# Two-layer graph network: the last steps re-timed, twelve tails shared out anew between VectorE and GpSimd

## The chip, the cores and the metric

The kernel runs on one core of a Trainium2 chip. Its engines are named as in the profile: PE (TensorE; PEld is its weight load), DVE (VectorE), ACT (ScalarE), POOL (GpSimd) and SP (SyncE, which here issues the DMAs). The metric is the device time of one execution in microseconds (us). All data are float32.

## The reference, cut to what matters

There are 128 batches of 128 nodes with 512 features; `adj` is a 128x128 matrix.

```python
# layer 0: A and C are the same product here, so max(relu(A + (C-A))) becomes a row maximum
A = adj @ x;  x = layernorm(x + relu(max_n(A) + b))
# layer 1, 8 heads of 64
q, k, v = split(x @ w_qkv)
attn = softmax(where(adj == 0, -inf, q @ k.T * 64**-0.5))
o = (attn @ v) @ w_proj + b_proj
x = layernorm(x + (o + layernorm(o) * gamma + beta))
```

## The kernel before, in words

Batches go in groups of four (32 groups, g), and a group in two pairs; q numbers the 64 pairs. The order of all work on each engine is written out by hand: every call is pinned, so the Python order is each engine's order, and each engine runs its own list strictly from first to last. The same holds for the DMA list on SP.

**Units.** The products with `w_qkv` and `w_proj` are done for a group at a time as units of seven block products instead of eight (class `Unit`): `product(i)` is one of the seven, 4 matmul calls on PE (8 rows in the trace, 1.73 us), into one of four PSUM banks, b1 to b4. `snap(k)` copies bank b1 to SBUF on ACT (L186, `u_qk`, `u_v`, `u_o`), and `result(half, col)` adds a bank and a snap on DVE (L192) into the unit's output, which frees the bank. There are two qk units, one v unit and one o unit a group. `seed` (L519) puts the projection's bias into a bank ahead of the products. `left_sums` / `run_sums` make the sums of blocks that the products take, on POOL.

**Attention of a batch.** `scores` (16 calls on PE into two PSUM banks, pss0 and pss1, or po and pa), `softmax_max` (scale and mask, L401, and row maximum, L413, on DVE), `softmax_exp` (ACT, L420, one head at a time), `softmax_div` (reciprocal L431 and product L77, DVE), `prob_transpose` (DVE, L441), `prob_write` and `prob_read` (two DMAs over DRAM that finish the transposition: `hop<-pu`, L450, and four `pT<-hop`, L461), then `attend` (PE) and `attend_copy` (ACT, L491).

**Tails.** A batch ends with two layer norms. Statistics: `bn` (L248, L249) on DVE and `finish_stats` (scale `rs` by a power on POOL, shift `sh`); for a few batches `scalar_stats` on ACT. `tail_inner` normalizes o (ACT); `tail_residual` does three POOL operations: times gamma, plus o, plus the layer's input row with beta, which was spilled to DRAM and is reloaded by `tail_reload` (L556) or `tail_reload_one` (L562). `tail_outer` normalizes again (ACT), and a store follows. For some of the last batches `fused_open` (two DVE operations, L619 and L77) and `fused_close` (one, L627) take the place of the inner normalization and of POOL's three.

**Steps.** A loop over pairs p (L772) does in each step: attend of the pair before, scores and softmax of pair p, two units interleaved, layer 0 of a later pair, tails of earlier pairs. It ends with p = LAST = 60. After it the last pairs are written out (L930 to L1136), with L = 127 the last batch. There `scores(L-5)`, `scores(L-4)` begin the first written step and `scores(L-1)`, `scores(L)` begin the third; the last four batches are projected one by one (`last_project`, PE, tile `pp`) with a copy of `w_proj` loaded over the qk weights (`last_load`, tile `wlast`, whose rest takes ten reloaded rows).

Of the kernel before, what the change touches and what calls it, by code (L numbers as in the profile page):

```python
# [9 lines left out]
F32 = mybir.dt.float32  # L10
AF = mybir.ActivationFunctionType
ALU = mybir.AluOpType
# [4 lines left out]
def kernel(  # L17
# [58 lines left out]
    def tt(eng, dst, a, b, op):  # L76
        pin(eng.tensor_tensor(dst, a, b, op))  # L77
# [84 lines left out]
    class Unit:  # L162
# [25 lines left out]

        def result(self, half, col):
            bank, k = {(0, 0): (2, 1), (0, 1): (3, 2), (1, 0): (4, 3), (1, 1): (3, 3)}[half, col]  # L190
            pin(
                nc.vector.tensor_tensor(  # L192
                    self.out[half, col], self.banks[bank], self.snaps[k], ALU.add
                )
            )
# [55 lines left out]
    def finish_stats(mv, keys, eng=None, fused=0):  # L251

        n = len(keys)
        if n == 0:
            return
        sh = small.tile([P, NC], F32, tag="sh", name=f"sh_{mv.name}")
        if eng is None:
            pin(nc.vector.tensor_scalar(sh[:, :n], mv[:, :n, 0], -1.0, None, ALU.mult))
        rs = small.tile([P, NC], F32, tag="rs", name=f"rs_{mv.name}")
        pin(nc.gpsimd.tensor_scalar(rs[:, :n], mv[:, :n, 1], EPS, None, ALU.add))  # L260
        tt(nc.gpsimd, rs[:, :n], rs[:, :n], mhalf.to_broadcast([P, n]), ALU.pow)
        if eng is None:
            tt(nc.gpsimd, sh[:, :n], sh[:, :n], rs[:, :n], ALU.mult)
        elif n > fused:

            part = slice(fused, n)
            pin(eng.tensor_scalar(sh[:, part], mv[:, part, 0], -1.0, None, ALU.mult))
            tt(eng, sh[:, part], sh[:, part], rs[:, part], ALU.mult)
        for k, key in enumerate(keys):
            stat_of[key] = rs[:, k : k + 1], sh[:, k : k + 1]  # L270
# [247 lines left out]

    def seed(unit, bank):  # L519
        cols = slice(HE, D) if bank == 3 else slice(0, HE)  # L520
        bias = bp_bc[:, cols].unsqueeze(1).to_broadcast([P, 2, HE])
        pin(nc.scalar.copy(unit.new_bank(bank), bias))
# [37 lines left out]
    def tail_reload_one(b, place):  # L560
        rs_[b] = place
        pin(nc.sync.dma_start(out=place, in_=spill[b // 2][:, b % 2]))  # L562
# [71 lines left out]
    def stats(name, *items, eng=None, fused=0):  # L634

        mv = small.tile([P, NC, 2], F32, tag="mv", name=f"mv_{name}")
        for k, (kind, b) in enumerate(items):
            bn({"o": o_of, "z": zs.get, "y": xs.get}[kind](b), mv, k)
        finish_stats(mv, items, eng, fused)
        return mv  # L640
# [131 lines left out]
    for p in range(LAST + 1):  # L772
# [117 lines left out]
        if p == 0:  # L890
            xsums = x_sums(1)
            run_sums(xsums[:3])
            second = qk_unit(1, 0)
        elif p == LAST:
            second = qk_unit(g + 1, 1)
        else:
            second = v_unit(g + 1) if ph else o_unit(g - 1)
# [21 lines left out]
        if p == 1:  # L919
            weight_sums(wp, 0, HE)  # L920
        if f is not None:
            one("y", xs, f)
# [6 lines left out]

    L = B - 1  # L930
    po_pa = ("po", "pa")
    pool = nc.gpsimd
# [4 lines left out]
    before.snap(3)  # L937
    attend_copy(L - 7)
    attend(L - 6, "pa")
    attend_copy(L - 6)  # L940
    seed(o_u, 2)
    scores(L - 5)
    scores(L - 4, po_pa)
    before.result(1, 1)
    tail_inner(B // 2 - 7)
    softmax_max(L - 5)
    before.result(1, 0)
    softmax_max(L - 4)
    o_u.product(1)
    o_u.snap(1)  # L950
    o_u.product(2)
    softmax_exp(L - 5)
    seed(o_u, 4)
    o_u.result(0, 0)
    before.product(3)
    before.result(0, 1)
    tail_residual(B // 2 - 7)
    softmax_exp(L - 4, range(4))
    o_u.product(6)
    scores(L - 3)  # L960
    scores(L - 2, po_pa)
    o_u.snap(2)
    seed(o_u, 3)
    softmax_exp(L - 4, range(4, H))
    softmax_div(L - 5)
    prob_move(L - 5)
# [3 lines left out]
    softmax_max(L - 3)  # L970
    softmax_exp(L - 3, range(4))
    o_u.snap(3)
    softmax_exp(L - 3, range(4, H))
    softmax_div(L - 4)
    prob_move(L - 4)
    softmax_max(L - 2)
    o_u.result(1, 1)
    o_u.result(1, 0)
    tail_outer(B // 2 - 8)
    tail_store(B // 2 - 8)  # L980
    tail_reload(B // 2 - 6)
    wlast, room = last_load()
    for t in range(L - 9, L + 1):
        tail_reload_one(t, room[:, t - L + 9])
    v_u.product(2)
    v_u.product(1)
    v_u.snap(1)
    stats("last_1", ("o", L - 9), ("o", L - 8), eng=pool)
    softmax_exp(L - 2, range(4))
    o_u.product(3)  # L990
    o_u.result(0, 1)
    v_u.result(0, 0)
    v_u.product(6)
    v_u.snap(2)
    softmax_exp(L - 2, range(4, H))
    for t in (L - 9, L - 8):
        tail_inner_one(t)
    tail_residual_one(L - 9)
    v_u.product(5)
    v_u.product(7)  # L1000
    stats("last_2", ("o", L - 11), ("o", L - 10), eng=pool)
    tail_residual_one(L - 8, [0])
    softmax_div(L - 3)
    prob_transpose(L - 3)
    prob_write(L - 3)
    v_u.snap(3)
    v_u.product(4)
    v_u.result(1, 1)
    softmax_div(L - 2)
    prob_transpose(L - 2)  # L1010
    prob_write(L - 2)
# [8 lines left out]
    scores(L - 1)  # L1020
    scores(L, po_pa)
    run_sums(o_sums(NG - 2))
    o_u = o_unit(NG - 2)
    seed(o_u, 2)
    for t in (L - 11, L - 10):
        tail_inner_one(t)
    softmax_max(L - 1)
    v_u.result(1, 0)
    v_u.product(3)
    softmax_max(L)  # L1030
    softmax_exp(L - 1, range(4))
    o_u.product(1)
    o_u.snap(1)
    seed(o_u, 4)
    softmax_exp(L - 1, range(4, H))
    v_u.result(0, 1)
    o_u.product(2)
    seed(o_u, 3)
    o_u.product(6)
    o_u.snap(2)  # L1040
    o_u.result(0, 0)
    softmax_exp(L, range(4))
    tail_residual_one(L - 8, [1, 2])
    stats("last_3", ("z", L - 13), ("z", L - 12), ("z", L - 9), eng=pool)
    o_u.product(5)
    o_u.product(7)
    softmax_exp(L, range(4, H))
    o_u.snap(3)
    o_u.product(4)
    softmax_div(L - 1)  # L1050
    prob_move(L - 1)
    o_u.result(1, 1)
    softmax_div(L)
    prob_move(L)
    tail_residual_one(L - 11)
    tail_residual_one(L - 10)
    tail_outer(B // 2 - 7)
    tail_store(B // 2 - 7)
    tail_outer_one(L - 9)
    last_seed(L - 3, "b2")  # L1060
# [3 lines left out]
    attend_copy(L - 2)  # L1064
    o_u.result(1, 0)
    mv = small.tile([P, NC, 2], F32, tag="mv", name="mv_last_4")
    bn(o_of(L - 5), mv, 0)
    bn(o_of(L - 4), mv, 1)
    finish_stats(mv, [("o", L - 5), ("o", L - 4)], pool)
    o_u.product(3)  # L1070
    o_u.result(0, 1)
    last_project(L - 3, wlast)
    for t, tag in ((L - 2, "b4"), (L - 1, "b3"), (L, "b1")):
        last_seed(t, tag)
# [3 lines left out]
    stat = scalar_stats(L - 8, L - 11)  # L1078
    finish_scalar_stats(stat)
# [5 lines left out]
    last_project(L, wlast)  # L1085
    mv = small.tile([P, NC, 2], F32, tag="mv", name="mv_last_5")
    keys = [("o", L - 3), ("o", L - 6), ("o", L - 7)]
    for k in (2, 1, 0):
        bn(o_of(keys[k][1]), mv, k)
    finish_stats(mv, keys, pool, fused=2)  # L1090
    fused_open(L - 3, mv[:, 0, 0:1])
    fused_open(L - 6, mv[:, 1, 0:1])
    fused_close(L - 3)
    tail_residual_one(L - 5)
    for t in (L - 8, L - 11):
        tail_outer_one(t)
    tail_inner_one(L - 7)
    mv = small.tile([P, NC, 2], F32, tag="mv", name="mv_last_6")
    keys = [("o", L - 2), ("z", L - 3), ("z", L - 10)]
    bn(zs[L - 3], mv, 1)  # L1100
    bn(zs[L - 10], mv, 2)
    fused_close(L - 6)
    bn(o_of(L - 2), mv, 0)
    finish_stats(mv, keys, pool, fused=1)
    fused_open(L - 2, mv[:, 0, 0:1])
    fused_close(L - 2)
    for t in (L - 3, L - 10):
        tail_outer_one(t)
    tail_residual_one(L - 4)
    mv = small.tile([P, NC, 2], F32, tag="mv", name="mv_last_7")  # L1110
    keys = [("o", L - 1), ("z", L - 2), ("z", L - 5), ("z", L - 6)]
    for k in (3, 2, 1, 0):
        bn((o_of if k == 0 else zs.get)(keys[k][1]), mv, k)
    finish_stats(mv, keys, pool, fused=1)
    fused_open(L - 1, mv[:, 0, 0:1])
    for t in (L - 2, L - 6, L - 5):
        tail_outer_one(t)
    tail_residual_one(L - 7)
    fused_close(L - 1)
    mv = small.tile([P, NC, 2], F32, tag="mv", name="mv_last_8")  # L1120
    keys = [("o", L), ("z", L - 1), ("z", L - 4)]
    for k in (2, 1, 0):
        bn((o_of if k == 0 else zs.get)(keys[k][1]), mv, k)
    finish_stats(mv, keys, pool, fused=1)
    fused_open(L, mv[:, 0, 0:1])
    for t in (L - 1, L - 4):
        tail_outer_one(t)
    fused_close(L)
    mv = small.tile([P, NC, 2], F32, tag="mv", name="mv_last_9")
    bn(zs[L], mv, 0)  # L1130
    finish_stats(mv, [("z", L)], pool, fused=1)
    mv2 = small.tile([P, NC, 2], F32, tag="mv", name="mv_last_10")
    bn(zs[L - 7], mv2, 0)
    finish_stats(mv2, [("z", L - 7)], pool)
    tail_outer_vector(L, mv[:, 0, 0:1])
    tail_outer_one(L - 7)  # L1136
# [41 lines left out]
```

## Time and profile before

| | us |
|---|---|
| median of 3 runs (lowest, highest) | 1964.25 (1963.17, 1967.03) |
| the profiled execution | 1965.37 |
| its span in the profile | 1963.5 |
| busy: PE, DVE, POOL, ACT | 1935.3, 1561.6, 1297.2, 1061.6 |
| SP's issuing of the ten row reloads (from 1899.24) | 7.50 |
| start of the last store's issue | 1960.35 |

Times in the profile count from the span's start. A timeline row gives start, duration, engine, line of the kernel, operation, tiles written and read with their shapes, how many such operations follow each other (x), and in brackets how long the engine was idle before, and what ended that. A row's duration on DVE or POOL includes the time in which the instruction had begun but waited inside its engine.

### The profile page before, as it was taken

To read this page: it belongs to the slowest core of one execution; us is meant where nothing else is said; L and a number is where in the kernel's file an instruction comes from. 1 tells how busy PE (TensorE), PEld (TensorE's weight loads), DVE (VectorE), ACT (ScalarE), POOL (GpSimd) and SP (SyncE) were. 2 spreads that over 40 slices of the span, in tenths; PEclk is the share of its full clock that TensorE was granted. 3 is DMA by queue.
4 is the path that set the end of the run, shared out by engine and by line. 5 is a ranking of instruction groups with operands and counts; after the bars stand their busy time and mean duration, and the time that the engine had idled before them with its cause. 6 is when DMAs were issued, how large, how long until landed. Compare 5 with 4: busy or idle time off the path is not lost.

```text
span 1963.5 us, 33034 instructions
## 1 busy us (share of the span) xinstructions
PE 1935.3 (99%) x11533; PEld 1637.7 (83%) x11533; DVE 1561.6 (80%) x2513; ACT 1061.6 (54%) x3084; POOL 1297.2 (66%) x827
## 2 busy tenths in 40 slices
PE   9999999999999999999999999999999999999995
PEld 6888888888888888888888888888888888888873
DVE  6767878878778778788787787787887877877876
ACT  3444654655555546546555555455465555554564
POOL 6336766767666767667676667676676766676748
PEclk9999999999999999999999999999999999999998
DMA  7647557576576676675675765765756657667554
GB/s 226 171 119 189 148 175 193 156 189 173 166 196 163 167 200 161 171 186 163 188 181 161 195 162 167 207 156 168 193 158 187 175 169 193 166 168 194 141 182 139
DMA packets 445653, 341.73 MB, mean 174 GB/s; under 512 B 276912, under 2 KB 378416, under 8 KB 445488
## 3 DMA queue, kind: packets, MB, share of 16 engines
q1 hardware_dynamic: 445056, 338.85, 63.3%
q8 instruction: 91, 1.49, 0.3%
q10 hardware_dynamic: 432, 0.79, 0.1%
q14 instruction: 74, 0.61, 0.1%
HBM read 172.82 MB, written 166.72 MB: 173 GB/s over the span
## 4 chain that ended last, share of the span: by engine, by line
PE 96%; DVE 2%; POOL 1%; ACT 1%; DMA 1%; issue 0%; SPq 0%; POOLq 0%; DVEq 0%; ACTq 0%
PE b_qk L74 40%; PE b_v L74 19%; PE b_o L74 18%; PE pss L74 6%; PE po L74 6%; PE pa L74 5%; PE pp L74 0%; DMA wlast<-spill 0%; ACT s L420 0%; POOL zl L77 0%; DVE s L401 0%; DVE s L77 0%; POOL rs_mv_last L77 0%; DVE st_mv_last L248 0%; DVE pu L441 0%
## 5 line engine op out<-in xcount | busy, mean ns | idle before, releaser
L74 PE MATMUL b_qk<-s_x,wqk 128*128 128x256 f32 x2048 | 473.2, 379 | 0.2 <-DVE v L192 0.2
L74 PEld LDWEIGHTS b_qk<-s_x,wqk 128*128 128x128 f32 x2048 | 389.0, 190 | 54.1 <-DVE v L192 0.6
L420 ACT ACTIVATE s<-s,nmax 128x128 f32<-128x128 f32 x1024 | 396.2, 391 | 5.7 <-DVE nmax L413 5.7
L74 PE MATMUL b_qk<-x1T,wqk 128*128 128x256 f32 x1536 | 358.9, 383 | 0.1
L74 PEld LDWEIGHTS b_qk<-x1T,wqk 128*128 128x128 f32 x1536 | 286.6, 190 | 45.3 <-issue 1.0
L77 POOL TENSOR_TENSOR z<-z,ga_bc 128x1024 f32<-128x1024 f32 x58 | 164.7, 2839 | 169.2 <-ACT z L274 169.2
L260 POOL TENSOR_SCALAR rs_mv<-mv 128x6 f32<-128x6 f32 (+2 forms) x61 | 14.6, 239 | 380.9 <-DVE mv L249 380.9
L77 DVE TENSOR_TENSOR s<-s,rec 128x1024 f32<-128x1024 f32 x128 | 252.0, 1969 | 4.4
L186 ACT COPY u_qk<-b_qk 128x512 f32<-128x512 f32 x192 | 112.4, 585 | 245.7 <-PE b_qk L74 244.7
L74 PE MATMUL b_v<-wv,s_x 128*128 128x256 f32 x1024 | 236.9, 379 | 0.0
L74 PE MATMUL b_o<-wp,s_o 128*128 128x256 f32 x992 | 229.7, 379 | 4.0 <-POOL s_o L77 2.6
L74 PEld LDWEIGHTS b_v<-wv,s_x 128*128 128x128 f32 x1024 | 194.4, 190 | 26.6
L74 PEld LDWEIGHTS b_o<-wp,s_o 128*128 128x128 f32 x992 | 188.2, 190 | 30.7 <-POOL s_o L77 3.0
L192 DVE TENSOR_TENSOR qk<-b_qk,u_qk 128x512 f32<-128x512 f32 x256 | 168.2, 676 | 56.6 <-PE b_qk L74 44.4
L401 DVE SCALAR_TENSOR_TENSOR s<-pss,mask 128x512 f32<-128x512 f32 x256 | 164.3, 684 | 59.0 <-PE pss L74 58.8
L77 POOL TENSOR_TENSOR x<-x,be_bc 128x1024 f32<-128x1024 f32 x64 | 181.3, 2834 | 33.4 <-DVE rec L431 27.3
L192 DVE TENSOR_TENSOR v<-b_v,u_v 128x512 f32<-128x512 f32 x128 | 87.1, 681 | 136.9 <-PE po L74 132.1
L420 ACT ACTIVATION_READ_ACCUMULATOR s<-s,nmax 128x1 f32 x1024 | 194.4, 190 | 0.0
L186 ACT COPY u_v<-b_v 128x512 f32<-128x512 f32 x96 | 56.2, 585 | 235.8 <-PE b_v L74 235.8
L186 ACT COPY u_o<-b_o 128x512 f32<-128x512 f32 x93 | 54.4, 585 | 237.0 <-PE b_o L74 237.0
L74 PE MATMUL b_v<-wv,x1T 128*128 128x256 f32 x768 | 176.2, 379 | 0.0
L74 PEld LDWEIGHTS b_v<-wv,x1T 128*128 128x128 f32 x768 | 145.9, 190 | 32.2 <-issue 13.6
(121 smaller groups left out, 3398.8 us busy)
## 6 DMA issues: line engine op xcount, KB each, us to landing
hop<-pu SPq DMA_DIRECT2D x128, 512.0 KB, 3.4
pT<-hop SPq DMA_DIRECT2D x512, 128.0 KB, 3.7
spill<-x SPq DMA_DIRECT2D x64, 512.0 KB, 4.8
x<-in_x_dram SPq DMA_DIRECT2D x62, 512.0 KB, 4.4
xhop<-xt SPq DMA_DIRECT2D x248, 128.0 KB, 2.2
x1T<-xhop SPq DMA_DIRECT2D x248, 128.0 KB, 3.9
xr<-spill SPq DMA_DIRECT2D x59, 512.0 KB, 3.6
out_dram<-xr SPq DMA_DIRECT2D x58, 512.0 KB, 4.1
```

Source lines behind the costliest of these rows:

```text
L74: pin(nc.tensor.matmul(*args, **kwargs))
L77: pin(eng.tensor_tensor(dst, a, b, op))
L186: pin(nc.scalar.copy(t, self.banks[1]))
L192: nc.vector.tensor_tensor(self.out[half, col], self.banks[bank], self.snaps[k], ALU.add)
L260: pin(nc.gpsimd.tensor_scalar(rs[:, :n], mv[:, :n, 1], EPS, None, ALU.add))
L401: nc.vector.scalar_tensor_tensor(s[:, par], pss[b][par], SCALE, mask.unsqueeze(1).to_broadcast([P, NP, P]), ALU.mult, ALU.add,)
L420: nc.scalar.activation(prob[b][:, i], prob[b][:, i], AF.Exp, bias=nmax[b][:, i : i + 1], accum_out=psums[b][:, i : i + 1],)
```

## The change

- The step of pair LAST is taken out of the loop and written out. In it `scores(L-5)`, `scores(L-4)` now come after `product(6)` of its first unit; `scores(L-3)`, `scores(L-2)` and `scores(L-1)`, `scores(L)` move into the next step. All softmax steps of these pairs follow them; `prob_read` is parted from `prob_write` and put later (for L-1 and L behind the store of pair 57).
- Reloads: pairs 59 and 60 go to a new tile `early` in the step of LAST, as whole pairs; pairs 61 to 63 go beside `wlast` as whole pairs. Before, ten single rows went there.
- Units of the last steps: `relay` copies bank b1 to a new bank b2 (ACT) and `product(2)` adds to it; `relayed` copies b2 to the output (ACT). They replace `snap(1)` and `result(0, 0)`, and bank 1 is seeded with the bias, bank 3 with the difference `bd` of the bias' halves, which POOL makes once in step p = 1.
- Tails: L-11, L-10 and L-7 become fused (DVE); outer statistics on ACT are now of L-9, L-8 and L-4 (before L-8 and L-11). The negated means are made on DVE (before, in the tails, on POOL). `stats` computes its items from last to first, everywhere. The order of the tails is new; L-7 no longer comes last.

```diff
-    def finish_stats(mv, keys, eng=None, fused=0):
+    def finish_stats(mv, keys, fused=0):
...
+        def relay(self):
+            pin(nc.scalar.copy(self.new_bank(2), self.banks[1]))
+        def relayed(self):
+            pin(nc.scalar.copy(self.out[0, 0], self.banks[2]))
...
     def seed(unit, bank):
-        cols = slice(HE, D) if bank == 3 else slice(0, HE)
-        bias = bp_bc[:, cols].unsqueeze(1).to_broadcast([P, 2, HE])
+        bias = {1: bp_bc[:, :HE], 3: bd}[bank].unsqueeze(1).to_broadcast([P, 2, HE])
...
-    def stats(name, *items, eng=None, fused=0):
+    def columns(name, *items):
         mv = small.tile([P, NC, 2], F32, tag="mv", name=f"mv_{name}")
-        for k, (kind, b) in enumerate(items):
+        for k, (kind, b) in reversed(list(enumerate(items))):
...
-    for p in range(LAST + 1):
+    for p in range(LAST):
...
+    first.product(6)
+    scores(L - 5)
+    scores(L - 4, po_pa)
+    softmax_exp(L - 6, range(4))
...
+    early = sb.tile([P, 4, D], F32, tag="x1T", name="early", bufs=2)
+    for q in range(2):
+        tail_reload_to(LQ - 4 + q, early[:, ds(2 * q, 2)])
...
+    prob_out(L - 2)
+    softmax_exp(L - 1, range(4, H))
+    v_u.relayed()
+    softmax_max(L)
+    o_u.result(1, 0)
+    o_u.result(0, 1)
...
+    for t in (L - 11, L - 10):
+        fused_open(t, mv2[:, t - L + 11, 0:1])
+    for t in (L - 11, L - 10):
+        fused_close(t)
+    tail_residual_one(L - 8)
+    o_u.product(5)
+    o_u.product(7)
+    o_u.snap(3)
+    last_seed(L - 2, "b1")
+    stats("last_3", ("z", L - 13), ("z", L - 12), ("z", L - 11), ("z", L - 10))
     attend(L - 3)
     attend_copy(L - 3)
     attend(L - 2, "pa")
     attend_copy(L - 2)
+    tail_outer(LQ - 6)
+    tail_store(LQ - 6)
+    prob_read(L - 1)
+    prob_read(L)
+    o_u.result(1, 1)
     o_u.result(1, 0)
...
+    stat = scalar_stats(L - 4)
+    finish_scalar_stats(stat)
+    fused_close(L - 1)
+    tail_outer_one(L - 4)
+    mv8 = stats("last_8", ("o", L), ("z", L - 1), fused=1)
+    fused_open(L, mv8[:, 0, 0:1])
+    tail_outer_one(L - 1)
+    fused_close(L)
```

`prob_out(b)` is `softmax_div`, `prob_transpose` and `prob_write`; LQ = 63 is the last pair.

## The prediction

> **What bounds the kernel now.** I read the page's busy shares and the chain that ended last, then the timelines of PE, DVE, POOL and ACT over the last 120 us, where the change lies, then its first 40 us.
>
> ```profile
> PE 1935.3 (99%) x11533; PEld 1637.7 (83%) x11533; DVE 1561.6 (80%) x2513; ACT 1061.6 (54%) x3084; POOL 1297.2 (66%) x827
> PE 96%; DVE 2%; POOL 1%; ACT 1%; DMA 1%; issue 0%; SPq 0%; POOLq 0%; DVEq 0%; ACTq 0%
> ```
>
> Up to 1891 us PE has no gap after the start; the change removes no matmul, so only gaps and the end can move. The PE timeline has four gaps:
>
> ```profile
> 1891.96 1.97 PE L74 MATMUL b_o<-wp,s_o 128*128 128x256 f32 x8 [1.04 <-DVE o L192]
> 1912.70 1.99 PE L74 MATMUL b_o<-wp,s_o 128*128 128x256 f32 x8 [2.60 <-POOL s_o L77]
> 1915.00 3.72 PE L74 MATMUL b_o<-wp,s_o 128*128 128x256 f32 x16 [0.31 <-ACT b_o L522]
> 1932.46 1.97 PE L74 MATMUL po<-pT,v 128*64 128x128 f32 x16 [3.73 <-DMA pT<-hop]
> 1934.36 12.74 PE L74 MATMUL pp<-wlast,oT 128*128 128x512 f32 x24
> ```
>
> They sum to 7.68 us. The last row shows a further cost: 24 projections in 12.74 us, where 8 took 3.45 in the chain (10.35 for 24). The granted clock was 0.83 and 0.76 in the last two stretches of the table by windows. After the last projection (1947.1) some 16 us remain, held by DVE with short waits for POOL:
>
> ```profile
> 1872.67 0.69 DVE L192 TENSOR_TENSOR qk<-b_qk,u_qk 128x512 f32<-128x512 f32 x1 [7.47 <-PE pss L74]
> 1940.27 0.70 DVE L248 BATCH_NORM_STATS2 st_mv_last<-pp 128x6 f32<-128x512 f32 x1 [3.13 <-PE pp L74]
> 1955.22 0.75 DVE L627 SCALAR_TENSOR_TENSOR z<-z,rs_mv_last,wlast 128x512 f32<-128x512 f32 x1 [1.80 <-POOL rs_mv_last L77]
> 1957.93 0.55 DVE L644 TENSOR_SCALAR z<-z,mv_last,rs_mv_last 128x512 f32<-128x512 f32 x1 [0.22 <-POOL rs_mv_last L77]
> 1959.51 0.81 ACT L274 ACTIVATE zl<-zl,sh_mv_last,rs_mv_last 128x512 f32<-128x512 f32 x1 [1.63 <-POOL sh_mv_last L77]
> ```
>
> DVE idles 7.47 us while PE works (room for a softmax), but is nearly dense from 1883 to 1900. The last store is that of L-7, issued at 1960.35.
>
> The price on which most hangs stands at the kernel's start, where DVE adds SBUF tiles while POOL adds SBUF tiles:
>
> ```profile
> 21.50 1.64 DVE L77 TENSOR_TENSOR s_x<-s_x,x1T 128x512 f32<-128x512 f32 x1
> 23.06 1.75 DVE L77 TENSOR_TENSOR s_x<-x1T 128x512 f32<-128x512 f32 x1
> 24.74 1.75 DVE L77 TENSOR_TENSOR s_x<-x1T,s_x 128x512 f32<-128x512 f32 x1
> 1930.62 0.69 DVE L77 TENSOR_TENSOR wlast<-o,wlast 128x512 f32<-128x512 f32 x1
> 1936.43 1.83 POOL L77 TENSOR_TENSOR zl<-zl,o 128x512 f32<-128x512 f32 x1
> ```
>
> The same DVE operation costs 0.69 us alone and 1.75 beside a busy POOL; POOL's usual 1.27 became 1.83 when a fused close (L627, 0.72 us from 1936.42) stood ahead of it.
>
> **What the Trainium skill says.** "SBUF — State Buffer", section "Who interferes with whom": a DVE instruction with two SBUF inputs and a GpSimd instruction that reads SBUF exclude each other, and the later one waits for the whole of the earlier. The five rows agree. That DVE's scalar_tensor_tensor waits as tensor_tensor does is not shown before the change; that POOL waits for it is. "TensorE: Matmul & The Clock Gate", section "What's actually happening": after an idle window of about 3.4 us PE drops to half clock until it has been busy for about as long. The trace agrees: after 3.73 us of idling the next projections take 0.85 us a row pair instead of 0.43.
>
> **The change, part by part.** I laid the instructions of both orders out engine by engine: each starts when its engine is free and what it reads is there, with the rows' durations. For the order before, this gives gaps of 1.0, 2.5, 0.6, 0.7 and 3.4 us against the measured 1.04, 2.60, 0.31, 0 and 3.73, so a gap is good to about 0.7 us.
>
> *Start.* `stats` now runs its items backwards. For batches 4 to 7:
>
> ```profile
> 28.34 3.31 ACT L292 ACTIVATE x<-x,r 128x512 f32<-128x512 f32 x4 [1.30 <-DVE r L289]
> 30.75 0.68 DVE L248 BATCH_NORM_STATS2 st_mv_second<-x 128x6 f32<-128x512 f32 x1
> ```
>
> DVE began batch 4 at 30.75; batch 7 is written at 31.65, so the four pairs (0.80 each) shift by 0.9 us. The result behind them ended at 34.8, and PE's product(3) at 34.90 needs its bank: **+0.8 us**. For batches 2 and 3 both rows are written (13.91) before DVE comes (14.04): 0. The new bd operation (128x256, under 1 us on POOL) hides beside PE: 0.
>
> *Softmax ahead.* scores(L-5), (L-4) (1.99 us of PE) move one step up, with 7.4 us of DVE per pair of maxima and first division; they fill DVE's 7.47 us hole. The layout leaves one gap, 0.6 us, behind ACT, where normalize(xr) and an exp stand ahead of snap(1). The gaps of 1.04, 2.60 and 0.31 go: **-3.95**. DVE is late next. From exp(L-3)'s end it owes two divisions with transposes (2 x 2.75), two maxima (2 x 2.44) and three results (1.9): 12.3 us, until o_u.result(0,1). PE has the rest of product(7) (1.5), scores 2.0 and four products (6.9), 10.4 us, and then v_u.product(5) needs the bank: gap 1.9. v_u.product(3) waits for a result after attend (0.8), the next product(4) for one behind the division of L, itself 0.9 us late from POOL's sums (0.7). **New gaps 4.0**: this part nets to nothing.
>
> *relay/relayed.* Three DVE results (0.68) go; three ACT copies (0.585) come, two seeds go. Where product(2) now waits for the copy, another product (1.73) covers it: 0. If that cover were gone, 3 x 0.6.
>
> *Reloads.* Ten 256 KB reloads become five of 512 KB, two of them a step sooner. SP spent 7.50 us issuing the ten; PE waited 2.60 through POOL's late residual, counted above. SP's hop writes get free; no DMA in the layout then holds PE until the last pair. There prob_read(L-1), (L) now stand on SP behind the store of pair 57, which waits for ACT's outer normalization and that for last_3. With last_3's statistics out at 1926.8 (worked from the next item): POOL 1.7, ACT 1.6, store 0.4, reads at 0.43 each, landing 3.3 after a pair's last: 1935.2 and 1936.9 against 1932.33 before. PE, at half clock, comes to them at 1935.9, so 0.5 us at most shows.
>
> *Tails.* L-11, L-10 and L-7 go from POOL (nine operations of 1.27) to DVE (three opens of 0.67+0.60, three closes of 0.67: 5.8 alone); one statistics pair goes to ACT (-0.8). L-11 and L-10 stand on DVE ahead of last_3 and of o_u.result(1,1), with POOL busy on L-9 and L-8: 6 x 1.75 = 10.5 us. From one instant (v_u.result(1,0)): DVE 0.6 + 10.5 + 4 x 0.80 + 0.7 = 15.0; PE 5 x 1.73 + 1.9 = 10.6. So PE's product(3) waits **4.4 us**. PE ended its attend at 1922.3 before; now 1922.3 + 0.8 - 3.95 + 4.0 = 1923.2, and product(3) starts at 1927.6 instead of 1922.3. The idle time is over 3.73, so the half clock comes here instead of at the attend.
>
> *End.* From 1927.6 DVE owes 2 results 1.2, 14 statistics pairs 11.2, 6 opens 7.6, 5 closes 3.4, 5 means 0.5, hand-overs 0.9: 24.8; waits for POOL at five of these 5.1, for the slow product(3) 1.1: 31.0, until 1958.6. The scale of L then waits 2.8 behind the scalar statistics of L-4 on POOL (ACT makes them after three outer normalizations); close, statistics, scale, outer 3.4: store at 1964.8. In the old order the last store was issued at 1960.35: **+4.4 us**.
>
> So the span is 1963.5 + 4.4 = 1967.9; that execution took 1965.37, 1.87 more than its span, and the median is 1964.25, 1.1 below it. From the median: **1968.6 us**. A measurement here can tell 0.2% (3.9 us) from no change.
>
> **Rivals.** (A) *PE sets the end, faster.* If DVE's fused operations do not wait for POOL, POOL's steps slip instead and the six take 3.9 us: the 4.4 us gap goes, and with it the half clock (12.74 - 10.35 and 1.0 at the attend: 3.4) and the 5.1 us of waits. PE ends near 1947.1 + 0.8 + 0 - 3.73 - 3.4 = 1940.8, and DVE, behind it by 1.5 to 3 us, ends 4 us sooner than now: 1960.3. It decides from a mean under 1.1 us for these six. For: no row shows scalar_tensor_tensor waiting. Against: tensor_tensor waits, and the skill makes it a matter of inputs.
> (B) *No difference.* If POOL is done earlier or half the operations pass, at 1.2 us each the six take 3.3 us less and the tail loses 2.5 less: 4.4 - 5.8 = -1.4, 1962.9.
> (C) *Worse.* DVE 3% slower over its 70 dense us (2 us) and the half clock reaching the later projections (2 us): 1972.6.
> That the softmax does not in fact come ahead, because its banks are held, would show as PE gaps near 1853; but the maxima that free the banks (L401) end at 1848.2 in that step already.
>
> **How the numbers follow.** The forecast case 0.44, C 0.10, B 0.25, A 0.21: faster 0.21, same 0.25, slower 0.54. The range goes from A's middle to C's middle, 1960.0 to 1973.0, leaving out half of A and of C. The forecast's own range is 1967 to 1971.
>
> **What would show it.** Right: PE gap of 4 to 5 us ended by DVE o before the last b_o product; DVE z/zl rows near 1.75 us ahead of it; product at double time after it; the close of L waiting over 2 us for POOL; a gap of about 0.8 us near 35 us. Wrong: those DVE rows near 0.7, or the last projection ending before 1944.

## The result, and the profile after

The changed kernel took **1969.3 us** (median of 10 runs, 1968.16 to 1970.5) against 1964.31 us for the kernel before in the same series (10 runs): ratio 1.0025, 95% interval 1.0015 to 1.0035. It is slower by some 5 us, a quarter of a per cent; 1968.6 was predicted, with a range from 1960.0 to 1973.0. The profiled execution of the changed kernel took 1970.11 us, its span is 1968.3 us.

The page after, busy times and the chain of work that ended last, shows the same number of matmuls, and a chain with 94% of PE where it had 96%, 3% of DVE where it had 2%, and less than half a per cent of POOL where it had 1%.

```profile
PE 1936.0 (98%) x11533; PEld 1638.4 (83%) x11533; DVE 1576.0 (80%) x2523; ACT 1061.9 (54%) x3087; POOL 1285.9 (65%) x808
PE 94%; DVE 3%; ACT 1%; issue 0%; DMA 0%; POOL 0%; SPq 0%; POOLq 0%; DVEq 0%; ACTq 0%
```

The timeline of PE in the last 102 us of the changed kernel (start, duration, operation, how many, in brackets PE's idle time before and what ended it):

```profile
1866.47 3.76 PE L74 MATMUL b_qk<-s_x,wqk 128*128 128x256 f32 x16 [0.51 <-ACT u_qk L186]
...
1900.92 3.72 PE L74 MATMUL b_v<-wv,s_x 128*128 128x256 f32 x16 [1.78 <-DVE o L199]
1909.12 1.99 PE L74 MATMUL b_v<-wv,s_x 128*128 128x256 f32 x8 [0.86 <-DVE v L199]
1913.33 3.69 PE L74 MATMUL b_o<-wp,oT 128*128 128x256 f32 x16 [0.48 <-DVE v L199]
...
1928.13 3.75 PE L74 MATMUL b_o<-wp,s_o 128*128 128x256 f32 x8 [4.03 <-DVE o L199]
...
1937.18 1.09 PE L74 MATMUL po<-pT,v 128*64 128x128 f32 x16 [1.15 <-DMA pT<-hop]
1939.45 1.09 PE L74 MATMUL po<-pT,v 128*64 128x128 f32 x16 [1.18 <-ACT oT L495]
1940.47 10.57 PE L74 MATMUL pp<-wlast,oT 128*128 128x512 f32 x24
```

The gaps of 1.04, 2.60 and 0.31 us of the order before are gone. In their place stand four small gaps (3.63 us in all), one of 4.03 us that DVE ends, and behind it a product at about half clock (3.75 us for eight rows; 1.99 in the row of 1909.12; the granted clock is 0.54 between 1926 and 1930 us). PE is through at 1951.0, and 14 us of DVE's and POOL's work follow.

DVE's timeline in the same kernel tells why the gap of 4.03 us is there and what the end waits for; three rows of POOL's timeline follow:

```profile
1913.70 1.76 DVE L624 SCALAR_TENSOR_TENSOR zl<-o,mv_last,ga_bc 128x512 f32<-128x512 f32 x1
1915.39 1.75 DVE L77 TENSOR_TENSOR xr<-o,xr 128x512 f32<-128x512 f32 x1
...
1920.42 3.44 DVE L632 SCALAR_TENSOR_TENSOR zl<-zl,rs_mv_last,xr 128x512 f32<-128x512 f32 x2
...
1931.91 0.69 DVE L199 TENSOR_TENSOR o<-b_o,u_o 128x512 f32<-128x512 f32 x1 [1.39 <-PE b_o L74]
...
1961.71 0.77 DVE L632 SCALAR_TENSOR_TENSOR z<-z,rs_mv_last,wlast 128x512 f32<-128x512 f32 x1 [2.60 <-POOL rs_mv_last L77]
```

```profile
1914.88 1.71 POOL L77 TENSOR_TENSOR zl<-zl,ga_bc 128x512 f32<-128x512 f32 x1
1916.67 1.60 POOL L77 TENSOR_TENSOR zl<-zl,o 128x512 f32<-128x512 f32 x1
1918.34 1.60 POOL L77 TENSOR_TENSOR zl<-zl,early 128x512 f32<-128x512 f32 x1
```

The opens and closes of L-11 and L-10, six operations, take about 1.75 us each (one starts every 1.68 us) while POOL has the residual of L-9 and L-8 under way, whose steps are longer too; the statistics of `last_3` and the result that PE needs stand behind them. The last DVE row is the close of L, held 2.60 us by POOL.

### The profile page after: what moved, and what is told of

The parts are those of the page before. It is cut to its first block, busy times and chain, and to the rows that moved or that the text cites. A ratio compares the mean times of both kernels' runs of the same rounds, so it can differ in the third digit from the quotient of the medians.

```text
span 1968.3 us, 33018 instructions
## 1 busy us (share of the span) xinstructions
PE 1936.0 (98%) x11533; PEld 1638.4 (83%) x11533; DVE 1576.0 (80%) x2523; ACT 1061.9 (54%) x3087; POOL 1285.9 (65%) x808
## 4 chain that ended last, share of the span: by engine, by line
PE 94%; DVE 3%; ACT 1%; issue 0%; DMA 0%; POOL 0%; SPq 0%; POOLq 0%; DVEq 0%; ACTq 0%
PE b_qk L74 39%; PE b_v L74 19%; PE b_o L74 18%; PE pss L74 6%; PE po L74 6%; PE pa L74 5%; DVE st_mv_last L255 0%; ACT s L424 0%; DMA x<-in_x_dram 0%; DVE s L77 0%; DVE zl L632 0%; DVE zl L624 0%; DVE pu L445 0%; DVE amax L291 0%; DVE xr L77 0%
```

## The experiments

All were run in five rounds with the kernel before beside them. Executions differ by up to 1.5 us before the first row that this change touches, so the table gives, beside the times, a **stretch** of each profile: from the start of PE's 16 products `b_qk<-x1T` near 31 us (32.07 in the changed kernel) to the start of the last store's issue (1965.02). All of the change lies within it but the order of the first statistics (near 13 us, where DVE waits for no row); a random start does not.

| kernel | median, us | kernel before beside it | ratio (95%) | stretch, us | stretch against the changed kernel |
|---|---|---|---|---|---|
| before | | | | 1928.93 | -4.02 |
| changed | 1969.3 | 1964.31 | 1.0025 (1.0015 to 1.0035) | 1932.95 | |
| statistics forward | 1968.73 | 1964.58 | 1.0021 (1.0013 to 1.003) | 1931.91 | -1.04 |
| L-4 behind L | 1966.88 | 1964.58 | 1.0014 (1.0007 to 1.002) | 1930.13 | -2.82 |
| POOL later | 1968.09 | 1964.58 | 1.0019 (1.0012 to 1.0027) | 1931.53 | -1.42 |
| PE kept busy | 1968.91 | 1964.58 | 1.0022 (1.0013 to 1.0031) | 1931.54 | -1.41 |
| PE early | 1967.68 | 1963.75 | 1.0021 (1.0014 to 1.0027) | 1930.88 | -2.07 |
| three edits | 1964.32 | 1963.75 | 1.0005 (0.9997 to 1.0013) | 1927.95 | -5.00 |
| three edits and POOL's order | 1962.21 | 1963.75 | 0.9992 (0.9984 to 1.0) | 1925.56 | -7.39 |
| the same, results before maxima | 1960.42 | 1963.75 | 0.9982 (0.9974 to 0.999) | 1923.62 | -9.33 |
| before, statistics reversed | 1965.62 | 1964.61 | 1.0007 (0.9999 to 1.0015) | 1927.54 | |
| changed, results before maxima | 1967.28 | 1964.61 | 1.0013 (1.0007 to 1.002) | 1930.06 | -2.89 |

One edit moves the median by less than the interval is wide, so the sizes below are read from the stretches, and the medians agree in direction. Each stretch is one execution, and the last section shows how far executions with the same gap differ. The profiled execution of the changed kernel was 0.8 us over its median, and differences of the ratios give savings that are 0.2 to 1.3 us smaller than those of the last column; PE early comes to 0.8 us by them, PE kept busy to 0.6. The profiled execution of before was itself 1.1 us over its median; differences to before are therefore taken from the ratios.

**Statistics forward.** Theory: DVE is late from the start by the wait for the last of four rows.

```diff
-        for k, (kind, b) in reversed(list(enumerate(items))):
+        order = list(enumerate(items))
+        for k, (kind, b) in order if name in ("first_2", "second", "third") else reversed(order):
```

> The changed kernel with the statistics of the three calls at the start (first_2, second, third) again in the order of their batches. Theory (the reversed order costs at the start and nothing between takes it up): DVE can begin with batch 4 when its row is written, 0.9 us before that of batch 7; PE's gap of 0.79 us at 36.48 us goes, and the end moves by as much, since neither PE nor DVE has room to spare later: span 1968.3 - 0.8 = 1967.5 us, about 1968.5 us in time. Rival (the start is taken up by a later wait): the gap goes at 36 us, but the time stays at 1969.3.

In the timeline of the changed kernel, first 40 us, the wait and the gap that follows from it:

```profile
32.34 0.69 DVE L255 BATCH_NORM_STATS2 st_mv_second<-x 128x6 f32<-128x512 f32 x1 [0.85 <-ACT x L296]
36.48 5.45 PE L74 MATMUL b_qk<-s_x,wqk 128*128 128x256 f32 x24 [0.79 <-DVE qk L199]
```

With the forward order the same PE row has no bracket:

```profile
34.39 5.45 PE L74 MATMUL b_qk<-s_x,wqk 128*128 128x256 f32 x24
```

The row starts 3.48 us into the stretch instead of 4.41, which is 0.93 us less (the bracket shows 0.79 of it), and the stretch is 1.04 us shorter. As expected: what is lost in the first 40 us is still lost at the end, since PE has next to nothing to wait for between (0.23 us, at 70 us).

**Statistics reversed in the kernel before.** The same line, put into the kernel before alone.

```diff
-        for k, (kind, b) in enumerate(items):
+        for k, (kind, b) in reversed(list(enumerate(items))):
```

> The kernel before with one line of the change alone: the statistics of a call to stats run from its last item to its first. Theory: at the start DVE waits 0.85 us for the row of batch 7 (as in the changed kernel), PE gets a gap of 0.8 us before the product behind the results, and the time rises by 0.8 us, ratio 1.0004; the later calls read rows that are all there. Rival (nothing): no such wait, ratio 1.0000. The times can hardly tell 0.8 us; the rows of the first 40 us can.

The timeline of that kernel has the same two waits:

```profile
32.56 0.69 DVE L248 BATCH_NORM_STATS2 st_mv_second<-x 128x6 f32<-128x512 f32 x1 [0.85 <-ACT x L292]
36.71 5.45 PE L74 MATMUL b_qk<-s_x,wqk 128*128 128x256 f32 x24 [0.79 <-DVE qk L192]
```

The waits are the line's doing. The time (ratio 1.0007, interval 0.9999 to 1.0015) agrees and cannot tell 0.8 us, as was expected.

**L-4 behind L.** What POOL does for L-4 stands behind the scales of L.

```diff
     stat = scalar_stats(L - 4)
-    finish_scalar_stats(stat)
     fused_close(L - 1)
-    tail_outer_one(L - 4)
     mv8 = stats("last_8", ("o", L), ("z", L - 1), fused=1)
+    finish_scalar_stats(stat)
     fused_open(L, mv8[:, 0, 0:1])
     tail_outer_one(L - 1)
+    tail_outer_one(L - 4)
```

> The changed kernel with the last three small steps of the scalar statistics of L-4 on POOL, and the outer normalization and store of L-4, put behind the scales of L. Theory: in the changed kernel the last close waits 2.60 us for rs of L, which POOL makes behind L-4's steps, and these wait for ACT; without that the last store is issued at 1965.02 - 2.60 = 1962.4, span 1965.7, time about 1966.7 us. Rival 1 (L-4 takes over as the last): ACT ends L-4's statistics at 1959.4, POOL's 0.3 + 0.9 for L and 0.9 for L-4 stand behind, then ACT 0.8 and the store 0.3: about 1962.6, so no more than 0.3 us less of a gain. Rival 2 (the close is held by DVE's own work or by PE): the wait shrinks but the end moves by less than 1 us.

DVE's timeline, the close of L:

```profile
1957.86 0.75 DVE L632 SCALAR_TENSOR_TENSOR z<-z,rs_mv_last,wlast 128x512 f32<-128x512 f32 x1 [0.46 <-DVE wlast L77]
```

The wait of 2.60 us is 0.46, which is 2.14 less, and the stretch is 2.82 shorter. Another 0.53 goes with a shorter wait of DVE for PE's slow product (0.86 us in this execution, 1.39 in the other), which the edit does not touch. L-4's store is issued at 1960.16, ahead of that of L at 1961.13, so L-4 does not take over. Rivals 1 and 2 are out.

**POOL later.** POOL's six residual steps are moved away from DVE's six operations, which stay.

```diff
-    tail_residual_one(L - 9)
     for t in (L - 11, L - 10):
         fused_open(t, mv2[:, t - L + 11, 0:1])
     for t in (L - 11, L - 10):
         fused_close(t)
-    tail_residual_one(L - 8)
...
     stats("last_3", ("z", L - 13), ("z", L - 12), ("z", L - 11), ("z", L - 10))
+    for t in (L - 9, L - 8):
+        tail_residual_one(t)
```

> The changed kernel with POOL's six residual steps of L-9 and L-8 moved behind the scales of last_3, so that POOL does nothing large while DVE makes the opens and closes of L-11 and L-10. Theory (it is POOL's steps beside them[...] that make six operations take 10.38 us; DVE is the bound): the six come to 4 x 0.67 + 2 x 0.60 = 3.9 us, 6.5 less; the result is there at 1921, before PE asks at 1924.1: the gap of 4.03 goes and product(3) takes 1.97 us, not 3.75; the last projection ends 4 to 7 us earlier. POOL is late next: six steps of 1.27 (7.6 us) now stand ahead of the scales of last_4 and last_5, the first closes begin at about 1935.5 instead of 1939.68, and waits for POOL grow; so the end comes 1 to 4 us earlier, span 1964 to 1967. Rival 1 (PE sets the end): the end follows PE, 5 to 7 us earlier, span 1961 to 1963. Rival 2 (these operations are slow by themselves, in SBUF, with or without POOL): they stay near 1.7 us, the gap stays at 4, and the end comes later by POOL's lateness.

DVE's timeline:

```profile
1913.17 1.76 DVE L624 SCALAR_TENSOR_TENSOR zl<-o,mv_last,ga_bc 128x512 f32<-128x512 f32 x1
1914.85 0.68 DVE L77 TENSOR_TENSOR xr<-o,xr 128x512 f32<-128x512 f32 x1
...
1916.72 1.40 DVE L632 SCALAR_TENSOR_TENSOR zl<-zl,rs_mv_last,xr 128x512 f32<-128x512 f32 x2
...
1937.67 1.76 DVE L632 SCALAR_TENSOR_TENSOR zl<-zl,rs_mv_last,early 128x512 f32<-128x512 f32 x1 [4.91 <-POOL rs_mv_last L77]
```

POOL's timeline, the end of its rest beside them:

```profile
1921.54 0.23 POOL L269 TENSOR_SCALAR rs_mv_last<-mv_last 128x4 f32<-128x4 f32 x1 [7.16 <-DVE mv_last L256]
```

The same operations come to 0.68 to 0.74 us, all but the first, which still meets POOL's last sum for the o unit (1913.11 to 1914.38). So it is POOL's work beside them and not the operation or its operands: rival 2 is out. PE's gap and its slow product are gone, and PE ends 4.1 us earlier in its stretch, but the end gains 1.42 us only. Where the rest went is the last row: POOL's steps now stand ahead of the scales that the first closes need, and DVE waits 4.91 us. Rival 1 (PE sets the end) would have had the end follow PE, 4.1 us here.

**PE kept busy.** Seven matmul calls (14 rows) without use in the gap of 4.03 us.

```diff
     prob_read(L)
+    warm = psum.tile([P, D], F32, tag="pss1", name="warm")
+    for _ in range(7):
+        pe(warm[:, :HE], lhsT=wp[:, 0, 0, :P], rhs=wp[:, 0, 1], start=True, stop=True)
     o_u.result(1, 1)
```

> The changed kernel with seven more matmuls of 128x256, into a bank that is free and whose result nobody reads, in PE's gap of 4.03 us, so that PE's longest idle time there is about 1.1 us. Theory (the half clock comes from the idle time, and DVE is the bound): product(3) takes 1.97 us instead of 3.75 and the next eight projections 3.45 instead of 4.36; DVE's wait of 1.39 us for product(3) goes, and as DVE is dense from there on the end comes 1.0 to 1.4 us earlier, span about 1967.1. PE itself gains nothing at its end, since its next attend waits for reads that land at about 1937. Rival 1 (PE sets the end): PE's end stays at 1951, since the reads hold it, and the end moves by less than 0.3 us. Rival 2 (product(3) is slow for another reason than the idle time): it still takes 3.7 us, and nothing moves.

PE's timeline:

```profile
1924.12 3.29 PE L74 MATMUL warm<-wp 128*128 128x256 f32 x14
1928.21 1.97 PE L74 MATMUL b_o<-wp,s_o 128*128 128x256 f32 x8 [0.81 <-DVE o L199]
...
1936.87 1.97 PE L74 MATMUL po<-pT,v 128*64 128x128 f32 x16 [3.27 <-DMA pT<-hop]
```

The product behind the gap, product(3), takes 1.97 us. PE itself gains nothing by it, since it now waits 3.27 us instead of 1.15 for the reads of L-1, and its last row starts at 1940.71; but DVE's wait of 1.39 us for the product is gone, and the stretch is 1.41 shorter. Here the half clock cost what DVE waited for it.

**PE early.** Both things that hold PE in the last 45 us are taken away: the two results go ahead of the statistics of `last_3`, and the reads ahead of the store of pair 57.

```diff
+    o_u.result(1, 1)
+    o_u.result(1, 0)
     stats("last_3", ("z", L - 13), ("z", L - 12), ("z", L - 11), ("z", L - 10))
...
-    tail_outer(LQ - 6)
-    tail_store(LQ - 6)
     prob_read(L - 1)
     prob_read(L)
-    o_u.result(1, 1)
-    o_u.result(1, 0)
+    tail_outer(LQ - 6)
+    tail_store(LQ - 6)
```

> The changed kernel with o_u.result(1,1) and result(1,0) ahead of the statistics of last_3 on DVE, and the reads of L-1 and L ahead of the store of pair 57 on SP: both things that hold PE in the last 45 us are taken away, while DVE keeps every operation. Worked from the rows of the changed kernel: the two results end 1.3 us after the last close (1923.9) less their overlap, so PE's product(3) starts near 1924.6 at full clock, its eight projections end near 1930, the reads have landed, and 24 projections (10.6 us) end near 1943.5 instead of 1951.0. Theory (DVE is the bound): DVE loses only its wait of 1.39 us for product(3); the end comes 1.4 us earlier, 2.5 at most if POOL's steps meet fewer of DVE's: span about 1966.5. Rival (PE sets the end): the end follows PE by 5 to 7.5 us, span 1961 to 1963.

PE's last row in that kernel's timeline:

```profile
1930.55 10.57 PE L74 MATMUL pp<-wlast,oT 128*128 128x512 f32 x24
```

PE ends at 1941.1, in its stretch 8.7 us earlier than in the changed kernel, and the end comes 2.07 us earlier. This is the plainest of the runs: three quarters of what PE gains is of no use, because DVE has the longer list.

The execution of "statistics forward" shows the same from the other side. Its last 24 projections ran partly at half clock:

```profile
1938.95 12.57 PE L74 MATMUL pp<-wlast,oT 128*128 128x512 f32 x24
```

There PE ends 1.6 us later in its stretch than in the changed kernel, DVE waits for none of these projections, and the end still comes 1.04 us earlier.

**Three edits together**: statistics forward, L-4 behind L, POOL later, with the diffs shown for each.

> The changed kernel with three edits that were run singly: statistics forward at the start, L-4's last steps behind the scales of L, POOL's residual of L-9 and L-8 behind last_3. Theory (the three costs are one after the other on the path of DVE): the gains add, 0.8 + 2.6 + 1.5 = 4.9 us, and the time comes to that of the kernel before, ratio 1.000 (within 0.0007). Rival (they share one slack): no more than the largest, 2.6 us and a little, ratio 1.0010 to 1.0013.

The stretch is 5.00 us shorter; the three alone gave 1.04 + 2.82 + 1.42 = 5.28, of which some 0.7 went with shorter waits for the slow product that the edits do not touch (by the ratios: 4.1 singly, 3.9 together). They lie one after the other on the path, as the theory has it, and the ratio is 1.0005, with 1 inside its interval. These three are enough to win back, within the interval, what the change loses against the kernel before. That nothing else is lost or gained is not shown: the swap at the end of this section saves time as well.

**POOL's order mended as well.** Added to the three edits: L-5's steps behind the scales of `last_5`, L-8's behind the closes of L-6 and L-3, the reads ahead of the store of pair 57.

```diff
-    for t in (L - 9, L - 8):
-        tail_residual_one(t)
+    tail_residual_one(L - 9)
...
-    tail_residual_one(L - 5, [0, 1])
...
     fused_open(L - 3, mv[:, 2, 0:1])
+    tail_residual_one(L - 5, [0, 1])
     fused_close(L - 6)
     fused_close(L - 3)
+    tail_residual_one(L - 8)
     stat = scalar_stats(L - 9, L - 8)
```

> The three edits together, and what was late next with POOL's steps moved: there the first close waited 4.91 us for POOL, which had the residual of L-8 (three steps, 4.5 us) and two steps of L-5 (2.5 us) ahead of the scales of last_5. Here L-5's steps stand behind those scales and L-8's behind the closes of L-6 and L-3, and the reads of L-1 and L stand ahead of the store of pair 57 (PE waited 2.89 us for them). Theory: of the 4.91 us of DVE's waiting 3.5 to 4.5 go, and the rest stays as waits beside POOL; below the kernel with three edits by 3.5 to 4.5 us, below the kernel before by about as much: ratio 0.998. Rival (ACT's statistics of L-9 and L-8, now later by three POOL steps, hold their outer normalization and POOL's next scales): a gain of less than 1 us over the three edits.

2.4 us came in place of 3.5 to 4.5. DVE's timeline shows what was given back:

```profile
1935.42 1.75 DVE L77 TENSOR_TENSOR early<-o,early 128x512 f32<-128x512 f32 x1
...
1943.74 0.78 DVE L632 SCALAR_TENSOR_TENSOR z<-z,rs_mv_last,wlast 128x512 f32<-128x512 f32 x1 [1.09 <-POOL rs_mv_last L77]
```

Of the 4.91 us, 1.09 is left as a wait for POOL's scales one round later, and five DVE operations in place of four now take 1.75 us beside POOL's steps (1.05 more): 4.91 - 1.09 - 1.05 = 2.8, which leaves 0.4 of the missing time untraced. The sign was right and the price of the new neighbours was left out.

**Results before maxima**, once in that kernel and once in the changed one alone. The maxima of L are pure DVE work that nobody waits for at once; the results free PE's banks.

```diff
-    softmax_max(L)
     o_u.result(1, 0)
     o_u.result(0, 1)
+    softmax_max(L)
```

> The kernel of e9_combined with the maxima of L (2.44 us on DVE) behind o_u.result(1,0) and (0,1) instead of ahead of them. PE's gaps of 1.78, 0.86 and 0.48 us (3.1 in all) lie behind those results: the first waits for o, the others for v, which DVE makes late. Theory (DVE's backlog of the softmax that was moved ahead makes these gaps): the first gap goes, the softmax of L is 1.3 us later and a gap of about 1.3 us for its bank or rows takes its place, so the end comes 1.5 to 2 us earlier than in e9_combined: ratio about 0.997. Rival (DVE is dense from there to the end whatever stands first, so that only the order changes): PE's gaps shrink and the end stays within 0.5 us of e9_combined.

> The changed kernel with the maxima of L behind o_u.result(1,0) and (0,1), and nothing else. In the changed kernel PE waits 1.78 us for the second of these results, which DVE makes behind the maxima, and DVE later waits 1.47 us for PE before a result of v (row at 1908.38): the first wait causes the second. Theory (PE and DVE lose the same time, once each): both waits go, another of about 1.1 us on PE for v comes, and everything behind, the gap of 4.03 us and the slow product included, moves 1.5 to 1.9 us earlier with no change of length: span about 1966.6. Rival (DVE is dense from 1885 on, as the prediction had it): PE's gap goes, the later one of 4.03 grows by as much, and the end moves less than 0.4 us.

In the changed kernel DVE has, 6 us after it made PE wait, a wait for PE of its own:

```profile
1908.38 0.69 DVE L199 TENSOR_TENSOR v<-b_v,u_v 128x512 f32<-128x512 f32 x1 [1.47 <-PE po L74]
```

With the new order alone, PE's gaps there are 1.11 and 0.23 us (3.12 before), DVE's wait of 1.47 does not occur, and in PE's timeline the large gap keeps its length and moves:

```profile
1925.01 3.00 PE L74 MATMUL b_o<-wp,s_o 128*128 128x256 f32 x8 [4.02 <-DVE o L199]
```

From PE's gap in step LAST (1866.47; 1865.41 here) that product starts 2.06 us earlier. That is the swap's own worth, a little over the 1.5 to 1.9 that were expected. The product takes 3.00 us this time instead of 3.75 and DVE's wait for it is 0.64 instead of 1.39, which the swap does not explain, and the stretch is 2.89 us shorter in all. The rival (DVE dense from 1885 on) falls. In the combined kernel, where that slow product is gone, the same swap gave 1.94 us, and with it a version that beats both: ratio 0.9982, interval 0.9974 to 0.999, which is 3.3 us less than the kernel before.

## Why the prediction was right, point by point

- **Start, +0.8.** Right: PE's row has a gap of 0.79 and starts 0.93 late, and both experiments on the line agree.
- **Softmax ahead, net nothing.** Right in the sum: gaps of 0.51, 1.78, 0.86 and 0.48 where 0.6, 1.9, 0.8 and 0.7 were worked out, against 3.95 removed. But the working took these gaps as the price of DVE's backlog and DVE as having no wait there. In fact DVE waits 1.47 us for PE at 1908.38, as a consequence of the first gap; 2.06 us could be had back by a swap of three lines.
- **Reloads.** No gap ends by POOL's late residual any more, as worked out. The reads behind the store of pair 57 cost PE 1.15 us, not 0.5: they were issued when expected, but at 0.54 us each for 0.43 (eight in 4.32), and landed after 3.9 (median) for 3.3. Another 1.18 us followed before the attend of L, which the profile puts down to a copy on ACT. To the end this was worth nothing: with PE kept busy that wait grew to 3.27 and the end came earlier all the same.
- **relay and bd at nothing.** No gap stands before a product(2), which agrees; the copies were not tried singly.
- **Tails.** The term on which most hung was 6 x 1.75 = 10.5 us; the rows add to 10.45 (they overlap a little: 10.19 from the first start to what follows). The Trainium skill ("SBUF — State Buffer", section "Who interferes with whom") says that a DVE instruction with two SBUF inputs and a GpSimd instruction that reads SBUF keep each other out. What no row of before showed, that scalar_tensor_tensor falls under it, holds: 1.75 us beside POOL, 0.74 with POOL quiet. The gap came to 4.03 for 4.4.
- **End.** The waits at five operations beside POOL were 4.8 for 5.1 (rows of 1.48 to 1.75 us between 1934.38 and 1943.04, in place of about 0.7), the wait of L's close was 2.60 for 2.8, the last store's issue 1965.02 for 1964.8 (this execution also started 0.65 later than that of before), and DVE's wait for the slow product 1.39 for 1.1.
- **The sum.** 4.4 us were forecast, 5.0 measured (interval 2.9 to 6.9). The mechanism was right, term by term; that the sum is only 0.7 us off in the median is in part luck. The 4.4 is counted from one execution of before, in which DVE waited 3.13 us for the projections at half clock; in the kernel with the reversed statistics that wait was 1.35, and counted from such an execution the same rows would have given a loss larger by some 1.8 us (an estimate from these two waits).
- **A reading.** The 0.43 and 0.85 us given for a row pair of the projections are the time of one row (24 rows take 10.57 us at full clock).
- **Rivals.** A (operations not delayed, PE setting the end) fell on the rows of 1.75 us, and its second half on PE early, where 8.7 us of PE were worth 2.07. B would have needed half of the operations to pass; all six took 1.72 us or more. C's mishaps did not come: the half clock reached only the first eight projections (4.36 us for 3.60), and DVE did not wait for them. Its price was too high as well: in "statistics forward" the last 24 took 12.57 us, and DVE waited for none.

Left open: whether the fused tails are worth their place on DVE at all. Giving L-11, L-10 and L-7 back to POOL in the new order was not tried.

## What to carry to other kernels

Before work is moved from GpSimd to VectorE, look at what GpSimd will be doing at that moment: where both had two-input operations on SBUF here, the moved operation cost more than it had (1.75 us, where POOL had taken 1.27), and the one behind it in VectorE's list paid. In a list that is written by hand, what another engine waits for goes ahead of what nobody waits for yet, small finishing steps of the last item go ahead of those of earlier items, and a loop over items runs in the order in which they are produced. A gap on the busiest engine is worth closing only to the extent that the engine which ends last waits for it.

## What was not expected of the hardware

The slow product behind PE's gap took 3.75, 3.57, 3.21 and 3.00 us in four executions with the same idle time ahead of it (4.02 or 4.03 us; the changed kernel, statistics forward, L-4 behind L, and results before maxima in the changed one), and DVE waited 1.39, 1.22, 0.86 and 0.64 us for it. In the order before, the 24 projections behind a gap of 3.73 us took 12.74 us, and behind one of 3.47 us, in the kernel with the reversed statistics:

```profile
1935.03 11.22 PE L74 MATMUL pp<-wlast,oT 128*128 128x512 f32 x24
```

DVE waited 3.13 us for the first of these projections in the one, and 1.35 in the other. The Trainium skill ("TensorE: Matmul & The Clock Gate", section "What's actually happening") has an account of such a spread: the window over which PE's activity is judged runs freely, so the phase of the work in it decides. The runs agree with it and do not prove it. By DVE's waits, that moves a stretch by up to 0.8 us among these four and by 1.8 between the two kernels with the order before, as much as one of these edits; so the one profile of before, with 12.74 us, is no good measure for a difference of that size.

Nor does one long idle time alone decide it. The 12.57 us of "statistics forward" stand behind idle times of 1.58 and 1.26 us with 16 short rows between them, and the granted clock is 0.50 between 1938 and 1942 us; in "PE kept busy" PE waited 3.27 us at the same place, the clock fell (0.60 between 1937 and 1941 us), but it was back before the 24 projections, which took 10.57.
